# The softmax mask of a windowed attention added in the tiling of the scores: eight matmuls a tile in place of two

## The chip, the core and the metric

The kernel runs on one core of a Trainium2 chip. Its time is the device time of one execution in microseconds (us), and of several runs the median counts. The core has a matmul engine (PE), which multiplies a stationary operand (the weights, brought in by a weight load, PEld in the profile) with a moving one and writes to PSUM; three engines for elementwise work and reductions (DVE, ACT and POOL); and SP, which here issues the DMAs.

## What is computed

The input is 2048 tokens of 128 features. The model is a sandwich: a transformer of six layers, added at half weight; a state space block (convolution, scan over the tokens with 16 states for each of 256 channels, gate); and the same transformer again. Each layer has a local attention with 16 heads of 64 and a gated feed-forward part. The attention is this:

```python
bk2, bv2 = (look(bk), look(bv))      # keys and values of the window before and of this one
mask = (it < jb) | (it > jb + w) | (jb == -1)          # w = 32
sim = jnp.einsum('bhwie,bhwje->bhwij', bq, bk2) * QK_SCALE
sim = jnp.where(mask, -jnp.finfo(sim.dtype).max, sim)
attn = jax.nn.softmax(sim, -1)
out = jnp.einsum('bhwij,bhwje->bhwie', attn, bv2)
```

A query sees 64 keys at most: those of its own window of 32 tokens and of the window before, no later key than itself and none more than 32 back. The first window has nothing before it.

## The kernel before

**Tiles.** The tokens are taken in tiles of 128. A layer runs over a segment of 1024 tokens, that is 8 tiles; there are two segments, six layers and two passes of the transformer, so 192 tiles in all. For one tile `project` (L374) makes queries and keys (x_ps), DVE and POOL rotate and normalise them, `turn` (L453) transposes them through PE (t_ps), `score` (L498) makes the scores (s_ps), ACT, DVE and POOL do the softmax, `average` (L595) makes the weighted inputs (z_ps), and `mix` (L619) multiplies them with a merged matrix of values and output projection (y_ps). The feed-forward part works on pairs of tiles (c_ps, v_ps, g_ps, a_ps, o_ps). `inputs` (L571) is a transpose of the tile's inputs (i_ps).

**Order.** The order of the work is written out by hand. The table `ORDER` (L65) gives each stage its lag in tiles and a position within the step, and `run` (L1173) goes through the steps, so that each engine has the stages of several tiles mixed in one fixed queue. The score stage S stands at 0.451 of a step, just behind EXW and PQ. In the middle of the run, from tile 48 on, the state space block's stages (`SPACE`, L79) are spread between the tiles, a round of 12 steps for each 256 tokens: these are the DVE scans (L1061), the ACT decays (L1050), the POOL products and the sums by PE (L1095).

**The score stage.** A tile holds four windows of 32 queries, and 16 heads. Two heads lie above each other in the 128 partitions of the transposed queries and keys, which makes 8 pairs (index c) and two halves of rows (index par: partitions 0 to 63, and 64 to 127). The scores of a tile fill two PSUM banks, one for each half: 128 queries by 8 heads by 64 keys. A score matmul (L517) takes one half, one pair and one window b: 64 rows (the features of the head) by 32 columns (the queries) as its weights, 64 keys as its moving operand. So the scores work in a tiling of 64 rows by 32 columns, in which the array has eight places, and go round these eight: 64 matmuls a tile, each of two passes in fp32, which are 128 records.

The mask goes ahead of them into the same banks, also by matmul (L506), and the scores are added to it. Its weights choose (`C_PICK`, L1307): the entry of row q and query i is 1 where i falls on q within its window. The moving operand (`C_MASK`, L1306) holds for row q the 64 entries of the mask, 0 or -1e25, and is read 8 times over, once for each pair, which gives 512 columns. Both lie in bf16, and both repeat every 32 rows over all 128 partitions. Before the change one matmul for each half does this with 32 of its rows and all 128 queries as columns, a tiling of 32 rows by 128 columns. For the first tile of the sequence (`st.tok == 0`) a second such matmul adds the mask of the missing window before.

What stands around the score stage on PE works with 128 columns: ahead of it i_ps (L574), behind it mostly c_ps (L662) or x_ps (L378), all in 128 by 128; z_ps (L602) has 32 rows by 128 columns.

Of the kernel before, what the change touches and what calls it, by code (L numbers as in the profile page):

```python
# [24 lines left out]
WIN = 32  # L25
# [101 lines left out]
class Stream:  # L127
# [370 lines left out]
    def score(self, g):  # L498

        nc, k, st = self.nc, self.k, self.at[g]  # L500
        st.s = self.bank2(("s_ps", g), 2).rearrange("p j (c k) -> p j c k", k=2 * WIN)
        for par in range(2):
            rows = slice(64 * par, 64 * par + 32)
            masks = [k.mask] if st.tok else [k.mask, k.mask0]
            for lhs, rhs in masks:
                nc.tensor.matmul(  # L506
                    out=st.s[:, par],
                    lhsT=lhs[rows],
                    rhs=rhs[rows].unsqueeze(1).to_broadcast([32, 8, 2 * WIN]),
                    start=lhs is k.mask[0],  # L510
                    stop=False,
                )
        for c in range(8):
            for b in range(4):
                for par in range(2):
                    rows = slice(64 * par, 64 * par + 64)
                    nc.tensor.matmul(  # L517
                        out=st.s[32 * b : 32 * b + 32, par, c, :],
                        lhsT=st.qt[rows, c, bass.ts(b, WIN)],
                        rhs=st.kt[rows, c, bass.ds(WIN * b, 2 * WIN)],  # L520
                        start=False,
                        stop=(c == 7),
                    )
# [870 lines left out]
```

## Time and profile before

| | us |
|---|---|
| median of 3 runs | 3309.81 (3309.39 to 3313.41) |
| span of the profiled execution, first to last instruction | 3308.2 |
| PE busy, matmuls | 3205.7 (97%) |
| POOL busy | 2907.1 (88%) |
| DVE busy | 2794.5 (84%) |
| ACT busy | 2551.3 (77%) |
| mask matmuls L506, 408 records | 77.4 busy, 0.384 for one |
| score matmuls L517, 24576 records | 286.9 busy, 0.225 for one |

The profiled execution's span is the time that all views of the profile are read against; the median stands 1.6 us above it. The profile's page has the busy time of each engine, the chain of work that ended last (followed back from the last instruction, at each step to what released it, or to the instruction before it on its engine), and the costliest groups of instructions by line. A group says, for instance, "32*128 32x512 bf16": weights of 32 rows by 128 columns, a moving operand of 32 partitions by 512 elements. The trace also gives each record with its start and length; the "single records" of the next section are these. A matmul is pipelined: its record runs on after the next one has begun, so that the lengths of a group do not add up, and the distance from start to start is what one matmul takes of PE's time. The granted PE clock is full in every part of the run.

### The profile page before, as it was taken

How to read it: one execution, taken by the hardware profiler on the slowest of the kernel's cores; microseconds unless marked ns; L12 is line 12 of the kernel's file. 1: busy time of each engine (PE TensorE's matmuls, PEld its weight loads, DVE VectorE, ACT ScalarE, POOL GpSimd, SP SyncE). 2: the span in 40 equal slices, each digit the busy share in tenths (PEclk: the TensorE clock that was granted, in tenths of full speed). 3: DMA queues.
4: the chain of work that ended last, by engine and by line, in shares of the span. 5: the costliest groups of instructions: out<-in, count | busy, mean ns of one | idle time of the engine just before them, and what ended most of it. 6: DMA issues, size and time to landing. Idle time of an engine off the chain costs nothing.

```text
span 3308.2 us, 97458 instructions
## 1 busy us (share of the span) xinstructions
PE 3205.7 (97%) x41936; PEld 2224.7 (67%) x41936; DVE 2794.5 (84%) x3524; ACT 2551.3 (77%) x4121; POOL 2907.1 (88%) x2317
## 2 busy tenths in 40 slices
PE   7999999999999999999999999999999999999998
PEld 4677677766666666666666666666666677677675
DVE  5778888888898989888989889898998888888884
ACT  5777777778778778787787877877877777777776
POOL 6999999998988989889888898898888889889884
PEclk9999999999999999999999999999999999999999
DMA  8221221221211121121211112111211111111000
GB/s 257 79 67 58 72 68 51 77 68 46 60 47 48 46 54 57 46 65 37 56 44 58 47 46 65 46 52 50 53 51 52 31 42 33 42 37 41 21 12 9
DMA packets 134494, 181.26 MB, mean 55 GB/s; under 512 B 13176, under 2 KB 91312, under 8 KB 127152
## 3 DMA queue, kind: packets, MB, share of 16 engines
q1 hardware_dynamic: 134064, 175.04, 17.8%
q8 instruction: 330, 5.41, 0.7%
q14 instruction: 100, 0.82, 0.1%
HBM read 138.75 MB, written 24.05 MB: 49 GB/s over the span
## 4 chain that ended last, share of the span: by engine, by line
PE 68%; DVE 12%; ACT 9%; POOL 8%; issue 2%; DMA 0%; SPq 0%; POOLq 0%; DVEq 0%; ACTq 0%
PE x_ps L378 16%; PE y_ps L623 15%; PE z_ps L602 8%; PE t_ps L459 7%; PE s_ps L517 6%; PE g_ps L704 3%; PE a_ps L704 3%; PE o_ps L750 3%; DVE da L1061 2%; POOL rot L446 2%; DVE rot L397 2%; DVE t L404 2%; PE y_ps L1095 2%; POOL rot L414 1%; ACT da L1050 1%
## 5 line engine op out<-in xcount | busy, mean ns | idle before, releaser
L414 POOL TENSOR_TENSOR rot<-rot,t 128x1024 f32<-128x1024 f32 x384 | 900.6, 2367 | 10.9 <-DVE rot L397 6.5
L378 PE MATMUL x_ps<-qk,r 128*128 128x512 f32 x1536 | 754.4, 614 | 29.0 <-ACT zt L614 10.3
L623 PEld LDWEIGHTS y_ps<-zt,m 128*128 128x128 f32 x6144 | 715.1, 192 | 63.5 <-ACT xc L673 36.7
L446 POOL TENSOR_TENSOR rot<-rot,rn 128x1024 f32<-128x1024 f32 x384 | 722.4, 1902 | 14.4
L623 PE MATMUL y_ps<-zt,m 128*128 128x128 f32 x6144 | 718.3, 275 | 5.2 <-ACT xc L673 3.4
L390 ACT ACTIVATE sq<-x_ps 128x1024 f32<-128x1024 f32 x384 | 393.2, 1024 | 276.0 <-DVE rot L397 230.2
L404 DVE TENSOR_TENSOR t<-x_ps,tab 128x1024 f32<-128x1024 f32 x384 | 467.8, 1218 | 162.1 <-PE i_ps L574 84.7
L557 POOL TENSOR_TENSOR pr<-pr,rs 128x1024 f32<-128x1024 f32 x192 | 365.2, 1902 | 192.6 <-DVE rs L553 154.5
L378 PEld LDWEIGHTS x_ps<-qk,r 128*128 128x128 f32 x1536 | 271.7, 190 | 361.2 <-issue 232.9
L397 DVE TENSOR_TENSOR rot<-x_ps,tab 128x1024 f32<-128x1024 f32 x384 | 467.5, 1217 | 18.8 <-ACT sq L390 18.3
L614 ACT COPY zt<-z_ps 128x1024 f32<-128x1024 f32 x384 | 368.9, 1010 | 140.8 <-PE z_ps L602 140.6
L420 DVE TENSOR_REDUCE ss<-sq 128x16 f32<-128x1024 f32 x384 | 466.6, 1215 | 8.1 <-ACT sq L390 5.4
L602 PE MATMUL z_ps<-pt,xw 32*128 32x512 f32 x3072 | 402.4, 614 | 2.6 <-DVE t L404 1.3
L541 POOL TENSOR_TENSOR pr<-pr,mx 128x1024 f32<-128x1024 f32 x192 | 365.4, 1903 | 25.8 <-ACT carry L1072 19.3
L459 PE MATMUL t_ps<-cs,rot 128*128 128x128 f32 x3072 | 370.9, 273 | 4.0 <-DVE sc L1082 1.9
L459 PEld LDWEIGHTS t_ps<-cs,rot 128*128 128x128 f32 x3072 | 343.9, 141 | 32.6 <-issue 10.7
L517 PEld LDWEIGHTS s_ps<-kt,qt 64*32 64x32 f32 x24576 | 255.8, 105 | 46.4 <-issue 45.4
L517 PE MATMUL s_ps<-kt,qt 64*32 64x64 f32 x24576 | 286.9, 225 | 0.0
L547 ACT ACTIVATE pr<-pr 128x1024 f32<-128x1024 f32 x192 | 203.1, 1058 | 105.1 <-POOL pr L541 104.3
L602 PEld LDWEIGHTS z_ps<-pt,xw 32*128 32x128 f32 x3072 | 146.4, 184 | 163.1 <-issue 130.0
L567 DVE STREAM_TRANSPOSE pt<-pr 128x1024 f32<-128x1024 f32 x192 | 237.0, 1234 | 2.1 <-POOL pr L557 2.1
L468 ACT COPY qt<-t_ps 128x1024 f32<-128x1024 f32 x192 | 193.9, 1010 | 56.8 <-PE t_ps L459 52.3
(144 smaller groups left out, 4839.3 us busy)
## 6 DMA issues: line engine op xcount, KB each, us to landing
bc<-bc SPq DMA_DIRECT2D x64, 512.0 KB, 5.4
tab<-tab SPq DMA_DIRECT2D x120, 256.0 KB, 2.6
qk<-in_wqk_dram SPq DMA_DIRECT2D x24, 1024.0 KB, 5.1
m<-m SPq DMA_DIRECT2D x24, 1024.0 KB, 5.3
tab<-in_tabs_dram SPq DMA_DIRECT2D x48, 256.0 KB, 2.9
xw<-xw SPq DMA_DIRECT2D x192, 48.0 KB, 3.1
m<-mst SPq DMA_DIRECT2D x6, 1024.0 KB
w<-w1s SPq DMA_DIRECT2D x18, 341.0 KB, 3.5
```

The costliest lines, as they stand in the source:

```text
L378: nc.tensor.matmul(out=x[:, j], lhsT=self.columns(g), rhs=st.w.qk[:, bass.ds(kind * INNER + j * 512, 512)], start=True, stop=True,)
L390: self.nc.scalar.activation(st.sq[kind], st.x[kind], AF.Square)
L397: self.nc.vector.tensor_tensor(st.rot[kind], st.x[kind], cos, ALU.mult)
L404: self.nc.vector.tensor_tensor(st.t2[kind].rearrange("p h (two c) -> p h two c", two=2), st.x[kind].rearrange("p h (two c) -> p h two c", ...
L414: self.nc.gpsimd.tensor_tensor(st.rot[kind], st.rot[kind], st.t2[kind], ALU.add)
L420: self.nc.vector.tensor_reduce(st.ss[:, kind, :], st.sq[kind], AX.X, ALU.add)
L446: self.nc.gpsimd.tensor_tensor(st.rot[kind], st.rot[kind], st.rn[:, kind, :].unsqueeze(2).to_broadcast([P, HEADS, DH]), ALU.mult,)
L459: self.nc.tensor.transpose(t_ps[:, c, :], flat[:, bass.ts(c, P)], self.k.ident)
L517: nc.tensor.matmul(out=st.s[32 * b : 32 * b + 32, par, c, :], lhsT=st.qt[rows, c, bass.ts(b, WIN)], rhs=st.kt[rows, c, bass.ds(WIN * b, 2 ...
L602: self.nc.tensor.matmul(out=st.z[b // 2][:, b % 2].rearrange("p (h q) -> p h q", q=WIN), lhsT=st.xw[rows, j, :], rhs=st.pt[rows, :, j, :], ...
L614: self.nc.scalar.copy(st.zt[:, 2 * half : 2 * half + 2].rearrange("p b h q -> p b (h q)"), st.z[half])
L623: self.nc.tensor.matmul(out=st.y_ps.rearrange("p (b q) -> p b q", q=WIN), lhsT=st.w.m[:, h // 2, h % 2, :], rhs=st.zt[:, :, h, :], start=( ...
```

## The change

The masks are added by eight matmuls a tile, one for each of four windows and two halves: 64 rows by 32 columns as weights, in the same places of the array as the scores that follow, and in the same order of places. The moving operand is the same, now of 64 rows. Since mask and weights repeat every 32 rows, each entry is summed twice, and a masked score gets -2e25 for -1e25. For the first tile of the sequence the second mask is added to its first window only, by two more matmuls. Weights and masks in memory are what they were, and nothing else in the kernel is touched.

```diff
-        for par in range(2):
-            rows = slice(64 * par, 64 * par + 32)
-            masks = [k.mask] if st.tok else [k.mask, k.mask0]
-            for lhs, rhs in masks:
-                nc.tensor.matmul(
-                    out=st.s[:, par],
-                    lhsT=lhs[rows],
-                    rhs=rhs[rows].unsqueeze(1).to_broadcast([32, 8, 2 * WIN]),
-                    start=lhs is k.mask[0],
-                    stop=False,
-                )
+        masks = [(k.mask, range(4))] if st.tok else [(k.mask, range(4)), (k.mask0, range(1))]
+        for (lhs, rhs), blocks in masks:
+            for b in blocks:
+                for par in range(2):
+                    rows = slice(64 * par, 64 * par + 64)
+                    nc.tensor.matmul(
+                        out=st.s[32 * b : 32 * b + 32, par],
+                        lhsT=lhs[rows, bass.ts(b, WIN)],
+                        rhs=rhs[rows].unsqueeze(1).to_broadcast([64, 8, 2 * WIN]),
+                        start=lhs is k.mask[0],
+                        stop=False,
+                    )
```

## The prediction, made before the result was known

> **What bounds the kernel now.** I read the page first: busy shares, then the shares of the chain that ended last.
>
> ```profile
> PE 3205.7 (97%) x41936; PEld 2224.7 (67%) x41936; DVE 2794.5 (84%) x3524; ACT 2551.3 (77%) x4121; POOL 2907.1 (88%) x2317
> ...
> PE 68%; DVE 12%; ACT 9%; POOL 8%; issue 2%; DMA 0%; SPq 0%; POOLq 0%; DVEq 0%; ACTq 0%
> ```
>
> PE, the matmul engine, is busy 97% of the span, but only 68% of the chain lies on it. So the stages differ, and I read the chain by windows. This is the window from 2790 to 2822 us, two tiles late in the run (columns: start, length, piece of the chain):
>
> ```profile
> 2797.44 1.93 PE z_ps L602 x16
> 2799.37 1.91 PE x_ps L378 x4
> 2801.28 0.11 PE i_ps L574
> 2801.39 0.32 PE s_ps L506 x2
> 2801.72 1.41 PE s_ps L517 x91
> 2803.13 1.91 PE x_ps L378 x4
> 2805.04 1.44 PE g_ps L704 x6
> ...
> 2818.67 1.42 PE s_ps L517 x91
> 2820.09 0.63 PE c_ps L662 x2
> 2820.72 1.29 PE x_ps L378 x3
> ```
>
> Here the chain is PE alone: each piece follows the last one, and PE waits for nobody. The masks (L506) and the scores (L517) are links of it, so whatever they lose or gain moves the end. In a window from 1499 us, where the scan stage runs beside the tiles, it is another picture:
>
> ```profile
> 1499.16 1.27 POOL y L985
> 1500.43 1.86 POOL pr L541
> 1502.29 1.24 POOL du L975
> ```
>
> There the scores of many tiles are off the chain. I went through the whole chain in windows of 30 us and counted the pieces named s_ps L506, one for each tile whose masks are a link: 37 before 840 us (50 tiles), 54 from 840 to 2640 us (101 tiles, the scan's stretch), 39 after that (41 tiles). That is 130 of 192.
>
> Next, the tile itself, from the timeline of PE between 506 and 509 us (start, length from the first start to the last end, group):
>
> ```profile
> 506.65 0.27 PE L574 MATMUL i_ps<-cs,r 128*128 128x128 f32 x1
> 506.86 0.39 PE L506 MATMUL s_ps<-masks 32*128 32x512 bf16 x2
> 507.17 1.49 PE L517 MATMUL s_ps<-kt,qt 64*32 64x64 f32 x128
> 508.59 0.70 PE L378 MATMUL x_ps<-qk,r 128*128 128x512 f32 x1
> ```
>
> And the two groups from the list of groups by form:
>
> ```profile
> L704 PE MATMUL a_ps<-q,w 128*128 128x256 f32 x384 | 99.4, 381 | 4.4 <-DVE t L404 4.4
> L506 PE MATMUL s_ps<-masks 32*128 32x512 bf16 x408 | 77.4, 384 | 0.0
> ```
>
> A matmul's record is longer than the time for which it keeps the next one away. In the single records, two matmuls of 256 fp32 columns in one tiling start 0.215 us apart, while each record lasts 0.381. The mask's record of 512 bf16 columns lasts 0.384, so it streams for about 0.215 + 0.003 = 0.218 us (no row shows this spacing for bf16: an estimate).
>
> **What a change of tiling costs.** In the single records, where one group follows another in the same tiling, the next matmul starts just one stream time later: 0.109 us after 128 fp32 columns, 0.215 after 256, 0.429 after 512. Where the tiling changes, it starts later: i_ps to masks 0.205 (0.096 more), z_ps to x_ps 0.517 (0.088 more), v_ps L684 to z_ps 0.309 (0.094 more), scores to what follows 0.145 against some 0.053 for 64 columns (0.092 more). From masks to scores it is 0.318 from the first mask's start, in nearly every tile: 0.218 of stream and 0.10 of change. The chain shows the same: four passes of x_ps take 1.91 us behind another tiling and 1.72 behind the same one (as behind c_ps, at 2790 us), a difference that holds the first weight load too. A dtype change leaves no mark of its own: 0.096 into bf16 masks, 0.094 into fp32 z_ps, both from 128 by 128 to 32 by 128.
>
> **The change, part by part.**
>
> 1. Removed: two weight loads and two matmuls of 32 rows by 128 columns a tile, side by side on the two halves of the rows, and one change of tiling, 0.10 us. A tile keeps two changes, into 64 by 32 and out of it; I leave both at their present price.
>
> 2. Added: eight loads and eight matmuls of 512 bf16 columns, each in its own eighth of the array. If they run side by side, they cost one stream, plus a weight load of 32 columns in front. In the scores' records the first eight matmuls start 7 ns apart, and the second on the same tile comes 80 ns after the first, later ones 56: so an uncovered load of 32 fp32 columns is some 0.024 us. The first mask then ends its stream 0.024 + 0.218 = 0.242 us after its start, and the first score, on the same eighth, can begin there, not at 0.318: 0.076 sooner. The other masks start 7 ns after each other, and so do the scores, so this stagger costs nothing if a score waits for its own eighth only; if the first one waits for all eight, it is 7 x 0.007 = 0.05 later.
>
> 3. Moved: the first scores' weights can load while the masks stream, where now they wait for the change of tiling: up to 0.024 us more. So 0.076 to 0.10; I take 0.09 us a tile. Twelve tiles (the first of the sequence in each layer, twice) also carry the second mask, now two matmuls more on one stream, before and after; nothing changes there.
>
> 4. Issue. PE gets six pairs of load and matmul more. Late in the score group pairs start some 0.0083 us apart, and that looks like a limit of issue, so six pairs could cost 0.05 us. I cost them at nothing: eight pairs need 0.06 us, and the masks stream for 0.218. The records give a sign that this cover holds: in tiles with four mask matmuls the scores start at 0.538, and their own pattern of starts is the same to 1 or 2 ns.
>
> 5. Other engines: the order of instructions and waits on DVE, ACT and POOL is unchanged; SP has two neighbouring DMA issues swapped in places. No wait is added and no buffer is held longer. The semaphore that released the first mask matmul still does.
>
> Does the eightfold overlap hold? No row has 512 columns in this tiling. The nearest is L517; the timeline from 507.20 to 507.29 us has
>
> ```profile
> 507.17 0.33 PE L517 MATMUL s_ps<-kt,qt 64*32 64x64 f32 x14
> ```
>
> Fourteen matmuls of 0.216 to 0.240 us fit in 0.33, seven or more in flight together, in both halves of the rows and all four column blocks.
>
> The Trainium skill speaks against this ("TensorE: Matmul & The Clock Gate", Part 3, The mechanism): a weight load overlaps running matmuls only where its group of rows is another one. By that rule the four masks of a half would run one after another, and the price would be that of rival A. L517 contradicts it here: loads for the second to fourth column block start 7 ns apart under a running matmul of the same half, so I follow the row.
>
> **Sum.** Late stretch and early stretch: 39 + 37 tiles x 0.09 = 6.8 us. POOL has room there (the table of windows has it busy 547 of 625 us from 2600 on), so nothing takes PE's place. In the scan's stretch a gain counts only until the runner-up path takes over, which no view prices; I take two thirds of 54, 36 x 0.09 = 3.2 us. Together 10.1 us: the execution's own span of 3308.2 goes to 3298.1. The median of the runs shown, 3309.81, stands 1.6 us above the span, so I forecast 3299.7 us. The forecast's own range: 0.05 us on 100 tiles (5) to 0.12 on all of 150 (18), so 3292 to 3305.
>
> **Rivals.**
>
> A. *The column blocks take turns.* Streams of 512 bf16 columns, four on the same rows, might not overlap as 64 fp32 columns do. Place: between first mask and first score. Four turns of 0.242 = 0.97 us for 0.32, 0.65 more a tile; on 130 tiles 85 us, on all 125: some 3395 to 3435. It decides as soon as the masks need over 0.32 us, that is when fewer than about six run at once. For it: no row of such streams here. Against: L517, and the two masks of today, which write two banks at the full width of 128 partitions side by side. Chance 9%.
>
> B. *The drain stays*, because bf16 masks and fp32 scores do not share the array. Then the first score starts after the last mask's start, its load and stream, and the old change: 0.05 + 0.242 + 0.10 = 0.39, 0.07 more than now; on 130 to 192 tiles 9 to 14 us: 3319 to 3324. For it: the only bf16 matmuls of this kernel always change tiling too, so the two are never seen apart. Against: 0.096 and 0.094 above. Chance 6%.
>
> C. *Nothing measurable.* The issue of six pairs eats half of the gain (0.04 left on 112 tiles, 4.5 us: 3305), or the scan's stretch and the first layers return nothing and the late one is all there is (39 x 0.09 = 3.5: 3306). For it: the 62 tiles off the chain. Against: the chain's two PE-only stretches. Chance 10%.
>
> That the change does not do what it says I rule out: the order of PE's program shows eight mask matmuls of 32 by 512 in each tile ahead of the scores.
>
> **Numbers.** The forecast has 75%, C 10%, A 9%, B 6%. This kernel's measurement can tell some 0.2%, 6.6 us, from no change, so faster means below 3303.2. A tenth of the forecast's own range lies above that: faster 68%, same 17% (with C), slower 15%. For 8 in 10 the range takes the forecast and C: 3291 to 3310.
>
> **What would show it.** In the late stretch a pair of tiles takes 30.74 us now, score to score (13.78 + 16.96); I expect 30.56. First mask to first score: 0.242 (0.32 or more speaks for B, near 1 for A). First to last score: 1.269 now; 1.245 if the first load is covered, up to 1.32 if issue bites. If the pair falls by 0.18 and the total by less than 7 us, the count of tiles on the chain was wrong. I would be wrong altogether if wide streams in one row half share something that 64-column fp32 streams do not fill.

## The result, and the profile after

The changed kernel takes 3321.42 us (median of 12 runs, 3314.92 to 3324.91) against 3312.88 for the kernel before on the same chip (12 runs, 3308.84 to 3315.71): a ratio of 1.0026, 95% interval 1.0019 to 1.0034. The change makes the kernel slower by a quarter of a per cent, where 0.3% faster was forecast; the time lies above the range. The profiled execution of the changed kernel has a span of 3320.0 us, 11.8 more than before. Two executions with a lower granted clock are left out of all ratios below: one of the kernel before (3373.19 us, clock 0.947), and of e8 the one that was profiled (3646.82 us, 0.849).

The page of the changed kernel, PE's busy time, its instruction queue, and the shares of the chain:

```profile
PE 3201.8 (96%) x43088; PEld 2237.7 (67%) x43088; DVE 2794.9 (84%) x3524; ACT 2553.1 (77%) x4121; POOL 2910.2 (88%) x2317
...
q8 instruction: 339, 5.55, 0.7%
...
PE 71%; ACT 11%; DVE 8%; POOL 7%; issue 2%; DMA 0%; SPq 0%; POOLq 0%; DVEq 0%; ACTq 0%
```

PE is busy 3.9 us less, in a span that is 11.8 us longer: it does its work sooner and stands still more. Queue q8 brings PE's instructions, in packets of 16,384 bytes; there are 339 where the kernel before had 330:

```profile
q8 instruction: 330, 5.41, 0.7%
```

No wait for another engine has grown enough to explain the span: of PE's waits above 0.15 us, those for ACT come to 40.7 us (38.4 before) and those for DVE to 41.3 (39.6), while those for nothing that the profile shows grow from 1.1 to 10.5. The late pair of tiles, by the chain of the changed kernel (start, length, piece):

```profile
2809.69 1.91 PE x_ps L378 x4
2811.60 0.11 PE i_ps L575
2811.71 0.34 PE s_ps L507 x8
2812.05 1.27 PE s_ps L518 x85
2813.33 1.92 PE x_ps L378 x4
2815.24 0.03 issue
2815.27 1.53 PE g_ps L705 x6
...
2820.37 1.30 PE a_ps L705 x6
```

Masks and scores are 1.61 us where they were 1.73. But g_ps, whose six matmuls took 1.44 us before, now takes 1.53 with 0.03 of issue ahead of it, while six matmuls of a_ps of the same shape take 1.30. In the kernel before they took as long, in the same pair of tiles as the prediction's g_ps:

```profile
2810.06 1.30 PE a_ps L704 x6
```

What the masks gave is handed back at g_ps. And the timeline of PE shows the change at work (start, length from first start to last end, group):

```profile
2811.44 0.27 PE L575 MATMUL i_ps<-cs,r 128*128 128x128 f32 x1
2811.64 0.41 PE L507 MATMUL s_ps<-masks 64*32 64x512 bf16 x8
2811.87 1.46 PE L518 MATMUL s_ps<-kt,qt 64*32 64x64 f32 x128
```

From the first mask to the first score it is 0.23 us (0.226 in the single records, 0.318 before). The masks run side by side, and the 0.10 us for the change of tiling between them and the scores is gone.

What is new stands in the list of PE's waits in the changed kernel (total us, times, longest), on rows whose releaser is "issue", that is, where PE waited for nothing that the profile shows:

```profile
PE s_ps L518 <- issue: 4.8, 2, 4.2
...
PE b_ps L254 <- issue: 3.2, 2, 1.9
...
PE x_ps L378 <- issue: 2.1, 2, 1.3
```

The longest of them, in the timeline of the changed kernel:

```profile
2015.84 0.41 PE L507 MATMUL s_ps<-masks 64*32 64x512 bf16 x8
2016.07 1.44 PE L518 MATMUL s_ps<-kt,qt 64*32 64x64 f32 x127
2021.74 0.26 PE L518 MATMUL s_ps<-kt,qt 64*32 64x64 f32 x1 [4.23 <-issue]
```

After 127 of 128 score records PE stands for 4.23 us. In the single records, numbered in order of time, loads, matmuls and semaphore waits together, this standstill and all others of its kind lie ahead of an instruction whose number leaves 193 when divided by 256: where one packet of q8 ends and the next begins. The transfer of the packet that PE wanted here began at 2019.40 us and landed at 2020.46, and PE went on 1.28 us later. So the standstills are **late instructions**.

I counted the places at such a boundary, from 100 to 3265 us, where more than 0.6 us lies between two starts of PE and the packet had landed at most 1.6 us earlier: 2 in the kernel before (1.4 us together), 9 in the changed one (13.0 us).

Why the boundary and the score stage meet: in the single records of the changed kernel, the transfer of the next packet begins, in half of the cases, between 0.3 us before and 1.2 us after the first instruction of the present one (median 0.8 after). It takes 0.9 us or more (median 1.0, longest 2.2), and no packet's first instruction began less than 1.2 us after its landing. So PE goes on without a stop as a rule if some 3 us lie between the first instructions of two packets (an estimate: the sum of the three). The rest of a tile is some 180 instructions in 12 us or more, but the score stage issues 272 in 1.6 us (260 in 1.73 before). If a packet begins some 9 to 24 instructions into the masks, the next one is wanted at or just after the stage's last score, before it can be there. The changed kernel has 12 such packets, and at seven of them PE stands still for over 0.6 us. The kernel before has eight (tiles 5, 12, 15, 66, 77, 95, 172 and 175) and no such standstill: its stage is 12 instructions shorter, so the next packet is first wanted some instructions later, among the x_ps matmuls, where one goes out every 0.2 us; it is 2.7 to 4.8 us from the first mask to that packet's first instruction.

### The profile page after: what moved, and what is told of

Its sections match the earlier page's. It is cut to its first block, busy times and chain, and to the rows that moved or that the text cites. A ratio compares the mean times of both kernels' runs of the same rounds, so it can differ in the third digit from the quotient of the medians.

```text
span 3320.0 us, 99763 instructions
## 1 busy us (share of the span) xinstructions
PE 3201.8 (96%) x43088; PEld 2237.7 (67%) x43088; DVE 2794.9 (84%) x3524; ACT 2553.1 (77%) x4121; POOL 2910.2 (88%) x2317
## 4 chain that ended last, share of the span: by engine, by line
PE 71%; ACT 11%; DVE 8%; POOL 7%; issue 2%; DMA 0%; SPq 0%; POOLq 0%; DVEq 0%; ACTq 0%
PE x_ps L378 17%; PE y_ps L624 16%; PE z_ps L603 8%; PE t_ps L459 8%; PE s_ps L518 6%; PE g_ps L705 3%; PE o_ps L751 3%; PE a_ps L705 3%; PE y_ps L1096 2%; POOL rot L446 2%; ACT da L1051 2%; PE s_ps L507 1%; ACT sq L390 1%; POOL rot L414 1%; DVE da L1062 1%
## 5 line engine op out<-in xcount | busy, mean ns | idle before, releaser
L390 ACT ACTIVATE sq<-x_ps 128x1024 f32<-128x1024 f32 x384 | 393.6, 1025 | 279.9 <-DVE rot L397 229.6
L459 PEld LDWEIGHTS t_ps<-cs,rot 128*128 128x128 f32 x3072 | 344.7, 141 | 34.1 <-issue 10.1
L518 PEld LDWEIGHTS s_ps<-kt,qt 64*32 64x32 f32 x24576 | 280.9, 105 | 12.1 <-issue 0.7
L535 DVE TENSOR_REDUCE mx<-s_ps 128x16 f32<-128x1024 f32 x192 | 233.0, 1214 | 8.5 <-PE s_ps L518 8.5
```

What stands on the lines that cost most here:

```text
L390: self.nc.scalar.activation(st.sq[kind], st.x[kind], AF.Square)
L459: self.nc.tensor.transpose(t_ps[:, c, :], flat[:, bass.ts(c, P)], self.k.ident)
L518: nc.tensor.matmul(out=st.s[32 * b : 32 * b + 32, par, c, :], lhsT=st.qt[rows, c, bass.ts(b, WIN)], rhs=st.kt[rows, c, bass.ds(WIN * b, 2 ...
```

## The experiments

The theory after the first look (theory 1): the score stage gained what it should; the second tile of each pair keeps its 16.96 us, since the bank pair that g_ps needs comes free only when ACT has read it; and late instruction packets, with the half clock that may follow a standstill, cost more than the rest gains. (Half clock: the trace lists stretches in which PE was granted 0.5 of its clock.) Rivals: that the new tiling itself slows PE or its clock, that the six further pairs cost their issue, and that the losses belong to places in the work. Every kernel was timed beside the kernel before on the same chip (medians 3311.5 to 3312.9). The late pair is the time from score to score in two neighbouring tiles late in the run. Places and half clock in the table are counted from 100 to 3265 us of each profiled execution; places are the late packets as counted above, and "standing" is the time from start to start over them.

| kernel | median us | ratio, 95% interval | late pair | places | standing us | half clock us |
|---|---|---|---|---|---|---|
| before | 3312.88 | 1 | 13.78 + 16.96 | 2 | 1.4 | 6.8 |
| changed | 3321.42 | 1.0026, 1.0019 to 1.0034 | 13.69 + 16.96 | 9 | 13.0 | 23.9 |
| e1 no masks | 3301.66 | 0.9963, 0.9950 to 0.9975 | 13.69 + 16.96 | 0 | 0 | 3.4 |
| e2 before, filled | 3327.62 | 1.0044, 1.0031 to 1.0057 | 13.80 + 16.96 | 8 | 11.6 | 3.4 |
| e3 changed, steered | 3308.30 | 0.9989, 0.9980 to 0.9998 | 13.69 + 16.96 | 3 | 2.0 | 3.4 |
| e5 before, filled and steered | 3316.62 | 1.0016, 1.0007 to 1.0025 | | 1 | 0.6 | 6.8 |
| e6 changed, shifted by 27 | 3309.75 | 0.9997, 0.9987 to 1.0006 | | 1 | 1.2 | 10.2 |
| e7 changed, shifted by 59 | 3319.39 | 1.0021, 1.0012 to 1.0030 | | 10 | 16.1 | 6.8 |
| e11 e3 with half squares | 3286.98 | 0.9924, 0.9912 to 0.9937 | 13.68 + 16.72 | 2 | 2.7 | 27.3 |
| e12 before with half squares | 3295.57 | 0.9952, 0.9938 to 0.9965 | 13.78 + 16.81 | 1 | 1.4 | 6.8 |

**e1: no masks at all.** The mask matmuls are left out; the first score of each place starts its bank.

```diff
-        for par in range(2):
-            rows = slice(64 * par, 64 * par + 32)
-            masks = [k.mask] if st.tok else [k.mask, k.mask0]
-            for lhs, rhs in masks:
...
-                        start=False,
+                        start=(c == 0),
```

> The kernel before, with the mask matmuls left out altogether (so the softmax runs over unmasked scores); the first score of each place starts its bank. The score burst is then 256 instructions long and a tile loses 0.318 us of PE time. Theory 1 (in every second tile PE meets a wait at the feed-forward matmuls g_ps, for PSUM banks that the queries' x_ps still hold, so a shorter score stage is worth something in the other tiles only): the steady pair of tiles goes from 30.74 us to some 30.35 (one tile by 0.32, the other by 0.07 at most), and the whole by 10 to 20 us, to 3293-3303. Rival (PE alone sets the pace of both tiles): the pair loses 0.63 us and the whole some 40, to about 3270.

It takes 3301.66 us, ratio 0.9963, in theory 1's range. Leaving out all of the 0.318 us a tile wins 10.5 us against the 3312.13 measured beside it, not the 61 that 192 tiles would make: the pair is 13.69 + 16.96, just as with the new masks, so the expected 30.35 for it was wrong. The chain of e1 in such a second tile:

```profile
2938.83 1.91 PE x_ps L378 x4
2940.74 0.12 PE i_ps L563
2940.87 1.21 DVE t L404
2942.08 1.14 DVE rot L397
2943.22 0.02 issue
2943.24 1.03 ACT sq L390
2944.28 0.14 issue
2944.41 1.53 PE g_ps L693 x6
```

Here is the path that holds the second tile: DVE and ACT read the queries' x_ps one after another (the two products with the tables, then the squares), and only then is its bank pair free for g_ps. Scores and masks are off the chain. And g_ps shows 1.53 us when it comes behind ACT, as in the changed kernel above. The first tile of the pair had no more than 0.09 us to give either: without masks its first y_ps load waits for ACT's copy of c_ps (xc), and y_ps takes 3.79 us where it took 3.57 before.

**e2: the old masks, but as many instructions.** Six matmuls of one column that add zero, in the scores' tiling, stand behind the old masks, so that the stage has the 272 instructions of the changed one.

```diff
+        for i in range(6):
+            rows, b = slice(64 * (i % 2), 64 * (i % 2) + 64), i // 2
+            nc.tensor.matmul(
+                out=st.s[32 * b : 32 * b + 32, i % 2, 0, 0:1],
+                lhsT=k.mask[0][rows, bass.ts(b, WIN)],
+                rhs=k.mask0[1][rows, WIN : WIN + 1],
+                start=False,
+                stop=False,
+            )
```

> The kernel before with its two masks in their old tiling, and behind them, in the scores' tiling, six matmuls of one column that add zero: the burst has as many instructions as in the changed kernel (272), with none of its mask tiling. Theory 1 (12 instructions more in the burst make the next block of 256 instructions arrive too late in some tiles, PE stands still for 0.5 to 4.5 us, and the granted clock falls behind it): stalls without a semaphore in or just behind the score stage, of about the same number (5 to 10 of over 0.5 us), more stretches at half clock than before, 3318 to 3328 us. Rival 2 (the masks in 64 by 32 tiling themselves lower the clock): only the issue of six pairs, 0.05 us in some 130 tiles, about 6 us, 3316 to 3319, no new stalls and a clock as before.

3327.62 us, ratio 1.0044: with nothing of the change but its number of instructions, the kernel is slower than the changed one. Seven of its eight standstills lie at tiles at which the changed kernel stands still. The timeline of e2, at the place shown above:

```profile
2016.15 0.39 PE L506 MATMUL s_ps<-masks 32*128 32x512 bf16 x2
2016.47 0.19 PE L515 MATMUL s_ps<-masks 64*32 64x1 bf16 x6
2016.51 1.45 PE L526 MATMUL s_ps<-kt,qt 64*32 64x64 f32 x127
2021.60 0.26 PE L526 MATMUL s_ps<-kt,qt 64*32 64x64 f32 x1 [3.64 <-issue]
```

Again one score record is cut off from the other 127. Theory 1's time is right and its clock is wrong: the half clock, 3.4 us here, is no part of e2's price, and the new tiling isn't either. The six pairs' own time is a small part: from the first mask to the line behind the scores it is 1.75 us, 0.02 more than before.

**e3: the changed kernel, steered.** 172 such pairs of zeros are put into the stages of 19 tiles, each so many that no packet begins 8 to 32 instructions into a later tile's masks.

```diff
+EXTRA = {
+    13: 6, 21: 7, 29: 7, 37: 7, 45: 3, 93: 5, 98: 9, 125: 14, 147: 13, 151: 9,
+    155: 7, 159: 9, 163: 10, 167: 11, 171: 11, 175: 11, 179: 11, 183: 11, 187: 11,
+}
...
+        for i in range(EXTRA.get(g, 0)):
```

> The changed kernel, with 172 matmuls of one column that add zero, put into the score stages of 19 tiles so that in no tile a block of 256 instructions ends in the first 8 to 32 instructions of the stage, where the trace of the changed kernel has its late blocks. Theory 1: no stall without a semaphore of over 0.6 us in or just behind a score stage, two to four stretches at half clock in place of six, 3302 to 3309 us: faster than the kernel before. Rival 2 (the tiling lowers the clock) or rival 3 (the stalls come from DMA traffic, whatever the position of the block): 3318 to 3326 us as in the changed kernel, stalls at other tiles.

3308.30 us, ratio 0.9989 (0.9980 to 0.9998). More instructions, and 0.37% less time than the changed kernel. The same tile in e3's timeline:

```profile
2009.77 0.41 PE L511 MATMUL s_ps<-masks 64*32 64x512 bf16 x8
2010.00 1.46 PE L531 MATMUL s_ps<-kt,qt 64*32 64x64 f32 x128
```

All 128 are together. From the fourth to the last tile's scores e3 is 7.4 us shorter than the kernel before; it loses 2.4 us ahead of that, where a packet is late in both and PE stands for 2.1 us in e3 and 1.2 before, and 3.1 after it.

**e4: g_ps later in the order.** To move g_ps off the wait, its place in ORDER goes from 0.715 to 0.735.

```diff
-    ("G", 6, 0.715), ("ZM", 4, 0.729), ("CK", 1, 0.745), ("CQ", 1, 0.746), ("TP", 3, 0.760),
+    ("G", 6, 0.735), ("ZM", 4, 0.729), ("CK", 1, 0.745), ("CQ", 1, 0.746), ("TP", 3, 0.760),
```

> The changed kernel with the feed-forward matmuls g_ps moved behind y_ps in PE's order (position 0.735 for 0.715). Theory 1 (the gain of every second tile is lost in g_ps's wait for banks): the steady pair goes from 30.65 to 30.40 us, since 0.19 us of wait is covered by the 3.6 us of y_ps, and the whole falls by 8 to 12 us against the changed kernel, less or more by the late instruction blocks, which move to other tiles: 3306 to 3316 us. Rival (another engine bounds the second tile at 16.96): the pair stays at 30.65, the wait turns up in another place of PE's order, and the whole stays at 3316 to 3325.

3366.45 us, ratio 1.0165 (1.0151 to 1.0179), and the late pair stays at 13.76 + 16.96: theory 1's numbers were wrong; the rival's wait in another place is there, but its time, 3316 to 3325, was wrong too. The chain of e4:

```profile
2932.86 2.20 PE z_ps L603 x16
2935.05 1.92 PE x_ps L378 x4
```

Now z_ps takes 2.20 us, not 1.93, I suppose because ACT does the gelu behind g_ps later; that isn't shown. The price doesn't lie here: of the 54.6 us by which e4 is longer than the kernel before from the fourth to the last tile's scores, all lie in the scan's stretch (tiles 50 to 151). This run doesn't tell what holds g_ps.

**e5: e2 and e3 together.** The old masks, the six pairs of zeros, and e3's pairs in the same tiles (the edit is against e2, and the table EXTRA is e3's).

```diff
-        for i in range(6):
-            rows, b = slice(64 * (i % 2), 64 * (i % 2) + 64), i // 2
+        for i in range(6 + EXTRA.get(g, 0)):
+            rows, b = slice(64 * (i % 2), 64 * (i % 2) + 64), i // 2 % 4
```

> The kernel before with six added 1-column matmuls a tile (as e2_before_fill, 3327.62 us) and with the same extra 1-column matmuls in 19 tiles as e3_after_steered has. Instruction for instruction it has the count of e3. Theory 1, blocks of 256 instructions that arrive late: e2 loses its price there, so about 12 us of e2's 15.5 us go: 3313 to 3317 us, ratio 1.000 to 1.0015, no standstill above 0.8 us without a semaphore in a score stage, and at most two half-clock stretches in the steady part. Rival, that the six further load and matmul pairs cost their own issue in each of 192 tiles: 3324 us or more, ratio 1.0035 or more.

3316.62 us, ratio 1.0016, inside theory 1's range: steering takes 0.28% of e2's 0.44%. Of the rest, 2.2 us lie ahead of the fourth tile and 4.5 behind the last tile's scores; over the 188 tiles between e5 is some 2.4 us longer than the kernel before, so six pairs behind the old masks cost 0.012 us a tile at most. And e5 and e3 hold the same number of instructions in each stage: the new masks are worth 0.9989 against 1.0016, some 9 us, of which up to 2.4 are the time of e5's own pairs.

**e6 and e7: one shift.** The changed kernel with 27, or 59, pairs of zeros in tile 0 alone. All later packets then begin 54, or 118, instructions earlier in the work.

```diff
+EXTRA = {0: 27}
```

> The changed kernel with 27 load and matmul pairs more in the stage of tile 0 alone, so that every later block of 256 instructions ends 54 instructions earlier in its stage. By the list of places, 6 tiles then have a block boundary 9 to 24 instructions into their masks, where the changed kernel has 12: tiles 46, 94, 107, 125, 169 and 184. Theory 1: the standstills above 0.6 us move to these tiles, and none stays at 41, 45, 102, 111, 115, 120 and 183; at about 1.1 us a late block (13 us less in e3 over 12 tiles) the time is about 3315 us, 3311 to 3319, ratio 1.001. Rival, that the lost time belongs to places in the work (the same tiles, other engines, the 512 KB loads): the same tiles stand still and the time is that of the changed kernel, 3319 to 3323.

> As e6_after_shift27 with 59 pairs more in tile 0: 17 tiles have a block boundary 9 to 24 instructions into their masks: 4, 8, 12, 31, 39, 43, 51, 55, 73, 100, 104, 113, 117, 122, 155, 159 and 181. Theory 1: standstills above 0.6 us at most of these tiles and at none of 41, 45, 102, 111, 115, 120, 183; at 1.1 us a late block about 3327 us, 3321 to 3333, ratio 1.0045, and above e6 by 6 us or more. Rival: the same places as in the changed kernel and 3319 to 3323, no difference from e6.

3309.75 and 3319.39 us: the two differ by 9.6 us, for 32 pairs of zeros in one tile. None of the changed kernel's nine tiles stands in either. In e6 only tile 184 does over 0.6 us, of the six listed; in e7 it is 12, 43, 55, 73, 117, 122 and 181 of the 17, tile 60 beside the list, and tiles 48 and 136 some way behind the stage. One of them, tile 117, in e7's timeline:

```profile
2052.45 0.70 PE L379 MATMUL x_ps<-qk,r 128*128 128x512 f32 x1
2054.27 1.45 PE L379 MATMUL x_ps<-qk,r 128*128 128x512 f32 x3 [1.12 <-issue]
```

The list was too long, and both times came out 5 to 8 us below the expected ones: a boundary 9 to 15 instructions into the masks often had its packet asked for 0.8 to 2.3 us before the masks began. Why isn't shown: PE's own steps ahead of the masks are the same at tiles 31 and 155 of e7, which don't stand, as at 73 and 117, which do (the longest two 0.52 and 0.43 to 0.45 us). The place is needed for most standstills and is not enough. The price: 9 places more and 14.9 us more of standing cost 0.0024 in the ratio, 8 us, 0.9 us each.

**e8: steered anew.** e6's shift, and 204 pairs (the expectation says 177) in 22 later tiles; the edit is against e6.

```diff
-EXTRA = {0: 27}
+EXTRA = {
+    0: 27, 10: 11, 14: 10, 22: 7, 30: 7, 38: 7, 46: 3, 47: 7, 51: 7, 60: 12,
+    69: 9, 74: 11, 105: 5, 110: 11, 137: 12, 157: 8, 161: 11, 165: 11, 169: 11, 173: 11,
+    177: 11, 181: 11, 185: 11,
+}
```

> The changed kernel steered anew: 27 pairs in tile 0 as in e6_after_shift27, whose first 50 us had no late block, and 177 pairs in 22 later tiles so that no block boundary lies 8 to 28 instructions into the masks. Theory 1: no standstill above 0.6 us in a score stage, the 2.9 us that e3_after_steered lost before its fourth tile are not lost, and the time is 3303 to 3308 us, ratio 0.9975 to 0.999. Rival, that e3 was a lucky placement: 3310 or more.

3309.74 us, ratio 0.9992 (0.9983 to 1.0001): above theory 1's range and just under the rival's. Which of its packets were late isn't known, since the profiled execution is the one left out. Steered versions lie at 0.999 of the kernel before, no better.

**e9 and e10: the squares first.** In e3, and in the kernel before, ACT's squares of the queries go ahead of DVE's second product.

```diff
-    ("NL", 1, 0.381), ("EXW", 1, 0.405), ("S", 2, 0.451), ("T2Q", 0, 0.454), ("T1Q", 0, 0.528),
-    ("XD", 2, 0.562), ("SQ", 0, 0.598), ("MX", 2, 0.633), ("F1", 5, 0.634), ("XN", 6, 0.647),
+    ("NL", 1, 0.381), ("EXW", 1, 0.405), ("S", 2, 0.451), ("T2Q", 0, 0.454), ("SQ", 0, 0.527),
+    ("T1Q", 0, 0.528), ("XD", 2, 0.562), ("MX", 2, 0.633), ("F1", 5, 0.634), ("XN", 6, 0.647),
```

> e3_after_steered (3308.3 us) with the queries' squares (ACT sq L390) put ahead of DVE's product with the cosines in the order of the work, so that the bank pair of x_ps comes free after DVE t and DVE rot alone, some 1 us earlier. Theory 1, that g_ps waits for this bank pair and so the second late tile keeps its 16.96 us: it falls to 16.83 to 16.90, the pair from 30.65 to 30.52 to 30.60, and the time by 2 to 8 us to 3300 to 3306. Rival, that another wait holds this tile (or that ACT then comes late with something else): 16.96 stays and 3306 to 3312.

> The kernel before with the same move of the squares. Theory 1, that in the kernel before PE's own path through masks and scores to g_ps (5.19 us) is exactly as long as the path over DVE and ACT: nothing is gained, the late tiles stay at 13.78 and 16.96 us and the time within 0.1% of the kernel before, 3309 to 3315. Rival, that the path over ACT bounds the kernel before as well: the second tile falls below 16.90 here too and the time to 3308 or less.

3467.28 and 3464.09 us (ratios 1.0474 and 1.0464): both expectations are wrong. The chain of e9 tells why:

```profile
3009.20 1.22 DVE t L408
...
3010.44 1.03 ACT sq L394
...
3011.50 1.24 DVE rot L401
...
3012.87 1.53 PE g_ps L718 x6
```

The three readers of x_ps run in turn in both orders, since a reader on the other engine waits for a semaphore that the one before it raises (in the records ACT's squares start 0.03 us after DVE's product has ended), so the pair comes free no sooner, and DVE now stands idle while ACT reads (270 us over the run, by the group of rot L401). Yet the two runs show one thing: where this path sets the pace in the first tile as well (14.58 + 17.09 us in both), old and new masks take the same time.

**e11 and e12: half of the squares.** ACT squares eight of 16 heads of the queries, in e3 and in the kernel before, and DVE's sums read that half twice, so that the path is shortened with no change of order; the other eight heads' squares are left out.

```diff
+        n = HEADS if kind else HEADS // 2
...
-        self.nc.scalar.activation(st.sq[kind], st.x[kind], AF.Square)
+        self.nc.scalar.activation(st.sq[kind], st.x[kind][:, :n], AF.Square)
```

> e3_after_steered (3308.3 us) in which ACT squares only half of the heads of the queries, and DVE's sums read that half twice: the squares of eight heads are left out, the rest and the order of the work stay. ACT sq L390 falls from 1.03 to about 0.52 us, so the bank pair of x_ps comes free some 0.5 us earlier, after DVE t and DVE rot as before. Theory 1, that g_ps waits for this bank pair, and so the second late tile could not use what its masks gave: it falls from 16.96 to 16.83 to 16.90 us, and the time by 2 to 7 us to 3301 to 3306. Rival, that another wait holds this tile: 16.96 (within 0.02) and 3306 to 3311.

> The kernel before with the same half squares (the squares of eight heads of the queries left out). Theory 1, that in the kernel before PE's own path to g_ps is as long as the path over DVE and ACT: the late tiles stay at 13.78 and 16.96 us (within 0.03), and the time at 3309 to 3313. Rival, that the path over ACT is the longer one there too: the second tile falls to 16.90 or less and the time by 2 to 7 us, as in e11, so that the tie explains nothing.

With the path half a microsecond shorter, the second tile falls in both: to 16.81 us with the old masks and to 16.69 or 16.75 with the new ones. The chains of e12 and of e11, in this order:

```profile
2940.90 0.32 PE s_ps L510 x2
2941.22 1.41 PE s_ps L521 x91
2942.63 1.91 PE x_ps L378 x4
2944.55 1.30 PE g_ps L708 x6
```

```profile
2939.54 0.32 PE s_ps L515 x3
2939.86 0.03 PE s_ps L524 x10
2939.89 1.36 PE s_ps L535 x78
2941.26 1.91 PE x_ps L382 x4
2943.17 1.29 PE g_ps L722 x6
```

In both g_ps takes 1.30 us and follows x_ps at once. (The ten records of L524 in e11 are steering pairs of this tile.) The times fall by more than the 2 to 7 us expected, some 21 us from e3 to e11 and 17 in e12. The path is worth something elsewhere too: of e12's 15.7 us from the fourth to the last tile's scores, 4.9 lie ahead of tile 50 and 7.5 in the scan's stretch. For the kernel before my expectation, that PE's own path is as long as the other, was wrong and its rival right: the path was 0.15 us longer there already. That makes the cause plainer. In the second tile of a pair PE had already to wait for ACT, so what the masks gave there could only lengthen that wait. With the wait taken away, the new masks win 0.09 us in the first tile and 0.06 to 0.12 in the second, 0.19 a pair, and 0.9924 against 0.9952 in all: some 9 us.

## Why the prediction was wrong

**What bounds the kernel: wrong for every second tile.** I read the late window as "PE alone" and wrote that "PE waits for nobody". The lines I showed hold the sign against it: g_ps L704 x6 at 1.44 us, where six matmuls of that shape take 1.30. A chain that goes along PE can hide a wait of 0.14 us inside a piece; it has to be compared with a piece of the same shape.

**Price of a change of tiling, removal and addition (parts 1 to 3): right.** First mask to first score was expected at 0.242 us and is 0.226; first to last score at 1.245 and is 1.242 (1.269 before). From the masks to the next line it is 0.117 us less, where I took 0.09 from a range of 0.076 to 0.10.

**Issue (part 4): the step that failed most.** "I cost them at nothing": in the stage itself that holds, since behind the old masks, where no stream covers them, such pairs add 0.02 us to it (e2), and behind the new masks the scores start sooner than forecast. But instructions also have to be brought. Six pairs more put 12 instructions more into a stage of 260, and in place of 2 late packets, 1.4 us of standing, there are 9, 13.0 us. e2 alone prices it, 1.0044 without any gain, and e3 takes it away. No part of the prediction looked at queue q8, though its line was on the page.

**Other engines (part 5): their order is unchanged, and their waits are not.** Only the sum's sentence "POOL has room there ... so nothing takes PE's place" speaks of it. POOL was the wrong engine to ask: DVE and ACT, busy 84% and 77%, carry the path that ends last in the second tile.

**The sum.** 0.09 us on 112 tiles, 10.1 us. Late pairs gain 0.09 us and not 0.18. Steered, the gain is 7.4 us over the 188 tiles between start and end: 2.6 us ahead of tile 50, 3.2 in the scan's stretch and 1.6 behind it, where I took 3.3, 3.2 and 3.5. So the sum is of the right size for a kernel whose instructions come in time, its late term is twice too large, and that the scan's term fits is luck, since no view gave its two thirds. Between the forecast span and the measured one lie 21.9 us: 13.7 that steering takes away, late packets and half clock together (e3's span is 3306.3), 5.5 that e3 too loses at the start and the end, and 2.7 that are missing from the gain.

**The Trainium skill's rule** ("TensorE: Matmul & The Clock Gate", Part 3, The mechanism) that a load overlaps running matmuls only in another group of rows was rightly set behind the row: here the loads of the eight masks, four to each half of the rows, start 3 ns apart while matmuls of both halves run, and the masks share one stream.

**Rivals.** A is refuted (0.226 us, not near 1), B as well (no change of tiling is paid between masks and scores); that the time lies in B's range, 3319 to 3324, is chance. C had half of the pair's gain about right in size, though not for the cause that it named, and the total wrong. That none of the rivals ended on the other side for the true cause is the fault of the list: both slow ones were about the array, none about what feeds it with instructions.

**What stays open.** The changed kernel's profiled execution has 23.9 us of half clock against 6.8 before. At half speed that is up to 8.5 us of its 11.8, and two of these stretches follow standstills; but e2 and e7 are slow with 3.4 and 6.8. The mean granted clock of each execution is on record, to 0.001. The changed kernel had 0.993 or 0.994 in ten of its 12 executions (3317.3 to 3324.9 us) and 0.996 in two (3314.9 and 3315.4); e3 at 0.996 took 3306.8 to 3311.1 us, and the kernel before, in the executions timed beside the experiments that count, had 0.996 or more. So of the 13 us between the changed kernel and e3 some 6 to 7 are left at the same clock, and the rest goes with the clock. Whether the late packets draw it down isn't shown: e11 has 27.3 us of half clock with 2 late packets.

One packet in each of the changed kernel, e2 and e7 came only 2.5 to 3.6 us into the stage, and these are the three longest standstills; in all three a transfer of 512 KB (bc) was issued 1.0 us before the masks began. It was not tried without that transfer, but the records go with it: in the changed kernel, after the first 100 us, the next packet's transfer begins more than 2 us into the present packet in 26 of 30 packets that begin 0.45 to 1.7 us after such an issue, and in 19 of the 302 others.

## What to carry to other kernels

Count the instructions of a burst, not only their time: where 260 instructions go out in 1.7 us, a dozen more can decide whether the next block of 256 is there, and a few idle instructions placed elsewhere can move the boundary out of the burst. Before a gain is put on the chain, compare each of its pieces with one of the same shape; a piece that is 0.14 us too long is a wait, and what is saved ahead of it is lost. If a change shows the expected effect in its stage and not in the total, look for PE's waits on nothing, and for where they stand in the order of instructions.

## What the runs showed of the hardware

- **Instruction blocks can be late without a branch.** Blocks of 256 PE instructions took 0.9 to 2.2 us to come (median 1.0, changed kernel), and PE began none less than 1.2 us after it had landed; standstills of up to 4.5 us (start to start) followed. The Trainium skill ("Runtime: NRT & Kernel Launch", Instruction fetch mechanics) describes the same blocks and calls the cost of crossing into one mostly hidden, since dispatch is slower than the refill. The score burst of about 6 ns an instruction shows where that ends.
- **The clock drops after partly idle windows.** The windows of the changed kernel around the long standstill (length, PE busy, further engines, granted clock):

```profile
2016.99:2020.40 3.41, 0.52 (x56) 0.37 (x38) 0.80 (x1) 1.02 (x1) 3.41 (x4) 0.95 0.58 117
2020.40:2023.81 3.41, 2.07 (x4) 0.84 (x4) 1.77 (x2) 0.51 (x1) 2.96 (x2) 0.50 0.01 1
2023.81:2027.23 3.42, 3.42 (x6) 1.53 (x5) 3.28 (x5) 0.50 (x1) 2.84 (x2) 0.56 0.02 5
```

  PE was busy 0.52 us of the first window, not idle. By the clock's own records half clock ran from 2020.03 us for 6.83 us, and in the 3.41 us ahead of it PE was busy for 0.90. Ahead of the five other such stretches between 100 and 3265 us it was busy for 1.15 to 2.18 us of 3.41. In the records of the two kernels such stretches last 3.41 us or 6.83, but for the one cut off by the end. The kernel before has them too (from 35, 63, 1025 and 1889 us, and at its end); the page's slices of 83 us, rounded to tenths, don't show them, and so "full in every part of the run" above was too coarse.
- **Eight bf16 streams of 512 columns share the array** in the tiling of 64 rows by 32 columns: their records start 3 ns apart, and all eight are over 0.41 us after the first start (changed kernel).
